# Window attention in pairs: copies placed between exponentials, variances by ScalarE squares with sums, small products at other pairs, indices from one row

## Chip, cores and metric

The kernel runs on one core of a Trainium2 chip. The metric is the device time of one launch in microseconds. Engines are named as in the profile: PE (TensorE), PEld (its weight loads), DVE (VectorE), ACT (ScalarE), POOL (GpSimd), SP (the queue that issues most DMAs).

## What is computed

A network of four layers works on 4 images of 256 channels by 64 x 64 positions, each layer as `x = x + layer(groupnorm(x))`. Layers 2 and 3 are state-space layers and are not touched. Layers 0 and 1 have the same form: a gated scan, then window attention with routing. Cut to the part that matters:

```python
def ssa(x_img, ...):                     # 8 x 8 windows of 8 x 8 positions, 8 heads of 32 channels
    q, k, v = split(xw @ qkv_w.T + qkv_b)
    logit = q.mean(2) * SCALE @ k.mean(2).T
    idx = top_k(logit, 4)                # 4 windows for each window
    k_g, v_g = kv[idx]                   # gathered: 4 x 64 keys and values
    attn = softmax(qh * SCALE @ kh.T)
    out = attn @ vh + lepe(v)            # lepe: a 3 x 3 depthwise convolution
    return out @ wo_w.T + wo_b

def _gn(v, G=32, eps=1e-5):              # v read as (batch, height, width, channels)
    g = v.reshape(B_, H_, W_, G, C_ // G)
    m, s = mean and variance of g over axes (1, 2, 4)
    return ((g - m) / sqrt(s + eps)).reshape(v.shape)
x = x + _L0_conv_ref(_gn(x), ...)
x = x + _L1_conv_ref(_gn(x), ...)
```

The array stands as (4, 256, 64, 64), so the axis that the group norm splits in 32 groups is the last spatial one: a group is a pair of columns over all 256 channels and 64 rows, for each image. A strip of 8 columns has four groups.

## The kernel before

Four images go one after the other. For each, `attention_layers` runs layer 0 and layer 1, and each layer has a scan phase (`scan_phase`), a small routing step and a window phase (`window_phase`). The image `x` stays in on-chip memory as 128 partitions by 2 halves of 4096. It is cut in 8 strips of 8 columns.

The window phase runs 32 pairs of windows, `i` from 0 to 31, with `sj, a = divmod(i, 4)`: strip `sj`, place `a` in it. The order on each engine is the order of the code: there is no scheduler, each engine takes its queue in turn, and semaphores are set where data or buffers demand it. The heads are handled in two halves, `h` 0 and 1, and the steps of one half are:

- `scores(i, h)` (L491): 32 small PE products into the PSUM tile `sc`. The tiles of `h` 0 and 1 alternate over two buffers.
- `smallest(i, h)` (L503): a VectorE minimum over `sc`, 128 x 1024, into `mn`.
- `exps(i, h)` (L514): four ScalarE exponentials of 128 x 256 with row sums, into `pr` and `sm`. A sum is read out by a second small instruction.
- `normalise(i, h)`: a VectorE reciprocal of the sums (L526) and four GpSimd scalings of `pr` (L529).
- `turn(i, h)` (L542): eight PE transposes into two PSUM tiles `pt`, of which there are only two buffers.
- `turned(h, 0)` on VectorE (L553) and `turned(h, 1)` on ScalarE (L555) copy them out to `pts` and so free the buffers.
- `values(i)` (L568): 64 small PE products of a pair into `ov`; `own_rows(i)` (L579) adds them to the image `vimg` on VectorE.

The pairs overlap: in the turn of the loop for pair `i`, PE works on scores of `i` (half 1) and `i + 1` (half 0), transposes of `i - 1` (half 1) and `i` (half 0), and values of `i - 1`. Besides these the loop places, between the steps:

- `project(s, m)` (L202, then `add`, L589) in the pairs with `a` 1 and 2, for the strip before: four PE products of 128 x 512 into the PSUM tile "mm", which has a single buffer in this phase, and a VectorE addition to `x`. Four other pairs (`i` 19, 20, 23, 24) hold a convolution for later queries (`query`) in the same buffer, moved out by ScalarE.
- `taps`: 51 GpSimd steps of the 3 x 3 convolution, two in each pair up to `i` 25. A tap is a product into a tile with tag "sq" (L223) and an addition (L226).
- `gather(i + 3)` and `indices(i + 4)`: eight SP transfers of 128 KB for a pair's keys and values into `kv` (room for four pairs), and two register loads, one for each window, from the routing result `idx` (L456).
- group-norm steps. `mids[i]` run ahead of the reciprocal of half 0, `ends[i]` at the end of the pair. In layer 0 they are the full norm `gn` of strips 0 and 1 for layer 1: sums on VectorE (L143), a PE product (`columns("pm")`, L134), a GpSimd subtraction (`center`, L151), a ScalarE square into a tile with tag "sq" (L159), a VectorE reduction (`reduce`, L163), a PE product (`columns("pv")`), and the scaling on GpSimd (`scale`, L174 and L178). In layer 1 they are `stats`: the same steps up to the variance, for layer 2, with the result kept in `gvar`. The last strip's statistics follow the phase.

The tag "sq" has one buffer, shared by these two lines:

```python
both = norm.tile([P, 2, 8, S], F32, tag="sq", name="tap", bufs=1)                  # L219, a tap
box["sq"] = norm.tile([P, 2, 8 * S], F32, tag="sq", name="gn_sq", bufs=1)          # L156, gn
```

Of the kernel before, what the change touches and what calls it, by code (L numbers as in the profile page):

```python
# [8 lines left out]
F32 = mybir.dt.float32  # L9
# [35 lines left out]
class Net:  # L45
# [33 lines left out]
    def attention_layers(self, x, w_drams, v_drams):  # L79
        tc, nc = self.tc, self.nc  # L80
        with ExitStack() as ctx:
# [40 lines left out]

            def gn(lay, s, psum, eng=nc.gpsimd, var=None):
                xs = x.rearrange("p (c h w) -> p c w h", c=2, w=S)[:, :, strip[s], :]
                box = {}

# [23 lines left out]

                def square():
                    xn = lay["xn"][s].rearrange("p c w h -> p c (w h)")
                    if var is None:
                        box["sq"] = norm.tile([P, 2, 8 * S], F32, tag="sq", name="gn_sq", bufs=1)  # L156
                    else:
                        box["sq"] = xn
                    nc.scalar.activation(box["sq"], xn, AF.Square)  # L159

                def reduce():
# [4 lines left out]

                def scale():
                    pv = box["pv"][:, 0:8]
                    if var is not None:
                        nc.vector.tensor_copy(var, pv.rearrange("p (g t) -> p g t", t=2)[:, :, 0])  # L170
                        return
# [20 lines left out]
                return g[0], both(g[1], g[2]), both(g[3], g[4]), both(g[5], g[6])  # L192


            def stats(s, psum, eng=nc.gpsimd):
                return gn(dict(xn={}), s, psum, eng, self.gvar[:, 4 * s : 4 * s + 4])


            def conv(psum, w, w0, src, m, tag="mm", **kw):
# [239 lines left out]
            def window_phase(lay, work, psum, idx, nxt):  # L439
# [8 lines left out]
                def queue(i, w):  # L448
                    return (nc.scalar, ET.Activation) if i < 2 and w else (nc.sync, ET.SP)

                def indices(i):
                    if i < n_pair:
                        regs[i] = []
                        for w in range(2):
                            p = window(i, w)
                            loads, win = nc.values_load_multi_w_load_instructions(  # L456
                                idx[p : p + 1, 0:TOPK], engines=[queue(i, w)[1]], min_val=0,
                                max_val=NW * NW - 1,
                                skip_runtime_bounds_check_because="places among 64 columns",
                            )  # L460
                            regs[i].append(win)
# [168 lines left out]
                for i in range(n_pair):  # L630
                    sj, a = divmod(i, 4)
                    add = evict = None
                    if i:
                        scores(i, 1)
                        turned(0, 0)
                        turned(0, 1)
                        turn(i - 1, 1)
                        smallest(i, 1)
                    for t in mids.get(i, ()):
                        t()  # L640
                    exps(i, 0)
                    if i == 0:
                        for f in early:
                            f()
# [61 lines left out]
            for i, lay in enumerate(layers):  # L706
# [15 lines left out]
                with tc.tile_pool(name=f"at_c{i}", bufs=1, reuse_waits="tile") as work, tc.tile_pool(  # L722
# [1391 lines left out]
```

## Time and profile before

| what | us |
|---|---|
| timed runs, median of 3 | 11982.6 |
| lowest and highest | 11980.29, 11991.5 |
| the profiled execution | 12008.04 |
| its span | 12006.0 |
| window phase of layer 0, four images, first to last minimum (L503) | 243.1, 244.8, 239.7, 243.8 |
| window phase of layer 1, four images, the same | 262.7, 262.6, 259.5, 264.0 |

The eight window phases take some 2000 us of 12000; the rest is scan phases and the state-space layers. All profile lines below are from one execution. A line of instructions has engine, line, operation, tiles, count, busy time and mean duration; a window line has the stretch, its length, busy time and count of each engine (PE, PEld, DVE, ACT, POOL), then the granted TensorE clock as a share of full speed, the share of the DMA engines and GB/s. A chain line has start, length and what was running; "issue" is time in which nothing that the profile shows was waited for.

### The profile page before, as it was taken

Reading aid. Unit: us, or ns where it says so; the run is one execution under the profiler, and the core shown is the slowest. Engines: PE = TensorE matmul, PEld = TensorE weight load, DVE = VectorE, ACT = ScalarE, POOL = GpSimd, SP = SyncE. Lnnn points to the kernel's source line nnn. Section 1 sums busy time; section 2 is a strip of 40 time slices with the busy share of each in tenths; the row PEclk is TensorE's granted clock in tenths of the full one; section 3 lists DMA queues with packets and bytes.
Section 4 is the critical chain, followed back from the end, with each engine's and each line's share of the span. In section 5 each row is a group of like instructions: output and inputs, shape, how many; then the busy total and the mean of one; then the engine's idle time right before and its main releaser. Section 6 shows DMA issues by size and latency. Waiting matters only on the chain. (4 is left out here: it accounts for less than half of the span.)

```text
span 12006.0 us, 192840 instructions
## 1 busy us (share of the span) xinstructions
PE 10107.7 (84%) x71104; PEld 5773.4 (48%) x71104; DVE 9878.0 (82%) x8386; ACT 6942.4 (58%) x12872; POOL 8890.2 (74%) x6082
## 2 busy tenths in 40 slices
PE   8998887777899788777789988878779998887777
PEld 4554554444455455444445545544444554554444
DVE  6667998998666799889866679989986667998998
ACT  4555554776455555577645555547764555554776
POOL 4666886898466688689846668868974666886897
PEclk9998998999999899899999989989999998998999
DMA  3344544554334455455433435545543343554554
GB/s 98 101 126 131 173 172 147 170 180 160 92 99 125 129 173 174 145 169 182 162 91 101 126 133 173 174 148 170 182 160 90 95 130 131 172 175 147 168 174 155
DMA packets 681294, 1742.11 MB, mean 145 GB/s; under 512 B 87680, under 2 KB 193680, under 8 KB 680096
## 3 DMA queue, kind: packets, MB, share of 16 engines
q1 hardware_dynamic: 675232, 1721.38, 44.5%
q8 instruction: 563, 9.22, 0.3%
q10 hardware_dynamic: 5120, 8.39, 0.3%
q14 instruction: 379, 3.10, 0.1%
HBM read 1601.51 MB, written 94.37 MB: 141 GB/s over the span
## 5 line engine op out<-in xcount | busy, mean ns | idle before, releaser
L958 POOL TENSOR_TENSOR hc<-h,cb 128x1024 f32<-128x1024 f32 x2056 | 4811.7, 2353 | 788.3 <-DVE h L952 349.3
L952 DVE TENSOR_TENSOR_SCAN h<-da,m_state,pb 128x1024 f32<-128x1024 f32 x1248 | 2919.9, 2340 | 163.9 <-DVE pb L946 3.3
L904 PE MATMUL y<-ident,hc 128*128 128x128 f32 x16384 | 2349.9, 291 | 416.7 <-POOL hc L958 347.7
L904 PEld LDWEIGHTS y<-ident,hc 128*128 128x128 f32 x16384 | 2046.9, 151 | 1141.2 <-POOL hc L958 598.6
L946 DVE TENSOR_TENSOR pb<-du,pb 128x1024 f32<-128x1024 f32 x1672 | 2024.3, 1211 | 128.6 <-PE pb L876 126.7
L888 ACT ACTIVATE da<-delta,m_v 128x1024 f32<-128x1024 f32 x1672 | 1899.1, 1141 | 135.2 <-DVE h L952 118.6
L876 PE MATMUL pb<-m_parts,pick 128*128 128x512 bf16 x3312 | 1081.2, 411 | 830.0 <-DVE h L952 771.7
L529 POOL TENSOR_SCALAR pr<-pr,sm,zero 128x256 f32<-128x256 f32 x2048 | 1139.2, 574 | 371.9 <-DVE sm L526 326.4
L876 PEld LDWEIGHTS <-pick 128*128 128x128 bf16 x3312 | 263.7, 101 | 1774.5 <-DVE h L952 971.8
L503 DVE TENSOR_REDUCE mn<-sc 128x4 f32<-128x1024 f32 x512 | 627.0, 1226 | 553.8 <-PE sc L491 553.3
L952 DVE TENSOR_TENSOR_SCAN h<-da,pb 128x1024 f32<-128x1024 f32 x424 | 969.7, 2287 | 55.6 <-DVE pb L946 1.5
L514 ACT ACTIVATE pr<-sc,mn 128x256 f32<-128x256 f32 x2048 | 941.3, 480 | 74.1 <-DMA kv<-kv_dram 57.0
L862 POOL TENSOR_TENSOR bb<-du,bb 128x1024 f32<-128x1024 f32 x376 | 889.2, 2365 | 119.7 <-DMA bb<-m_cd 112.6
L542 PE MATMUL pt_ps<-ident,pr 128*128 128x128 f32 x4096 | 719.3, 301 | 125.9 <-POOL pr L529 111.2
L555 ACT ACTIVATE pts<-pt_ps 128x512 f32<-128x512 f32 x512 | 306.5, 599 | 772.3 <-PE pt_ps L542 771.2
L952 DVE TENSOR_TENSOR_SCAN h<-dap,m_state,bb 128x1024 f32<-128x1024 f32 x288 | 672.1, 2334 | 68.4 <-ACT dap L888 47.9
L202 PE MATMUL conv_ps<-att_y,att_wb 128*128 128x512 f32 x1536 | 684.1, 595 | 4.4 <-DVE gn_mean L149 4.4
L542 PEld LDWEIGHTS pt_ps<-ident,pr 128*128 128x128 f32 x4096 | 482.9, 148 | 310.1 <-POOL pr L529 255.8
L491 PE MATMUL sc<-kv,q_swap 32*64 32x128 f32 x8192 | 602.5, 290 | 3.1 <-DMA kv<-kv_dram 2.7
L888 ACT ACTIVATE dap<-delta,m_v 128x1024 f32<-128x1024 f32 x376 | 419.7, 1116 | 307.8 <-DVE h L952 238.6
L491 PE MATMUL sc<-kv,att_y 32*64 32x128 f32 x7168 | 568.5, 288 | 6.8 <-DVE att_y L270 2.8
L491 PEld LDWEIGHTS sc<-kv,att_y 32*64 32x64 f32 x7168 | 431.3, 140 | 140.1 <-ACT pr L514 78.0
(295 smaller groups left out, 18095.2 us busy)
## 6 DMA issues: line engine op xcount, KB each, us to landing
cb<-m_cd SPq DMA_DIRECT2D x2048, 512.0 KB, 3.9
kv<-kv_dram SPq DMA_DIRECT2D x1984, 128.0 KB, 2.8
bb<-m_cd SPq DMA_DIRECT2D x376, 512.0 KB, 5.3
kv_dram<-kst SPq DMA_DIRECT2D x128, 256.0 KB, 3.5
kv_dram<-vn SPq DMA_DIRECT2D x128, 256.0 KB, 4.1
q_swap<-att_y SPq DMA_DIRECT2D x96, 256.0 KB, 4.1
m_pe<-in_pe_dram SPq DMA_DIRECT2D x32, 512.0 KB, 5.9
out_dram<-yo SPq DMA_DIRECT2D x64, 256.0 KB, 2.5
```

Of the source, the lines that this page charges most:

```text
L202: nc.tensor.matmul(ps, w[:, k, w0 + m * P : w0 + (m + 1) * P], src[:, k], start=(k == 0), stop=(k == 1),)
L491: nc.tensor.matmul(sc[h][b * 64 : b * 64 + 64, r, w, m, :], (own(sj, m) if r == b else swap[sj % 2][:, m])[rows, 2 * a + w], kv[i, w][rows ...
L514: nc.scalar.activation(t[:, g].rearrange("p j r t -> p r j t"), sc[h][:, :, g // 2, g % 2, :].rearrange("p r (j t) -> p r j t", j=2), AF.E ...
L529: nc.gpsimd.tensor_scalar(t[:, g], t[:, g], s[:, g : g + 1], self.zero, ALU.mult, ALU.add)
L542: nc.tensor.transpose(pt[h][j][:, g, :], t[:, g, j].rearrange("p r t -> p (r t)"), self.ident,)
L862: nc.gpsimd.tensor_tensor(pb[i], slots[i][0]["du"], pb[i], ALU.mult)
L876: nc.tensor.matmul(pb[i][:, ss], self.pick[:, n : n + 1].to_broadcast([P, P]), blk["parts"][:, ss], start=True, stop=True,)
L888: nc.scalar.activation(da[i], blk["delta"], AF.Exp, scale=blk["a"](n))
L904: nc.tensor.matmul(blk["y"][:, ss], t[:, ss], self.ident, is_transpose=True, start=(n == 0 and ss.start % NT == 0), stop=(n == DS - 1 and ...
L946: nc.vector.tensor_tensor(pb[i], blk["du"], pb[i], ALU.mult)
L952: nc.vector.tensor_tensor_scan(h[i][:, ss], da[i][:, ss], pb[i][:, ss], state, ALU.mult, ALU.add)
L958: nc.gpsimd.tensor_tensor(hc[i][:, ss], h[i][:, ss], cb[i][:, ss], ALU.mult)
```

## The change

Five things are altered, all of them inside the window phase or at its end.

1. The four exponentials of a half are split in two and two. Two are queued ahead of the copy `turned(h, 1)` on ScalarE, two behind it.
2. `normalise(i, 1)` is placed ahead of `own_rows(i - 1)`, so that the reciprocal stands first on VectorE.
3. `stats` (layer 1) is written anew: after the mean, four ScalarE squares with bias and sum take the place of subtraction, square and reduction; the squares themselves go to a tile with tag "xn" and are not used.
4. The steps of `gn` and `stats` are planned at other pairs.
5. From pair 4 on the indices are loaded from one row `row` with eight entries a pair by one register load. Two transfers ahead of pair 0 make that row by way of DRAM.

```diff
-            def stats(s, psum, eng=nc.gpsimd):
-                return gn(dict(xn={}), s, psum, eng, self.gvar[:, 4 * s : 4 * s + 4])
+            def stats(s, psum):
...
+                def mean():
+                    box["mean"] = self.small.tile([P, 4], F32, tag="gn_mean", name="gn_mean")
+                    nc.vector.tensor_scalar(
+                        box["mean"], box["pm"][:, 0:4], -1.0, None, ALU.mult
+                    )
+
+                def squares():
+                    box["s2"] = self.small.tile([P, 4], F32, tag="gn_s2", name="gn_s2")
+                    sq = norm.tile([P, 2, 8, S], F32, tag="xn", name="gn_sq")
+                    for g in range(4):
+                        two = slice(2 * g, 2 * g + 2)
+                        nc.scalar.activation(
+                            sq[:, :, two], xs[:, :, two], AF.Square,
+                            bias=box["mean"][:, g : g + 1], accum_out=box["s2"][:, g : g + 1],
+                        )
+
+                def variance():
+                    nc.vector.tensor_copy(self.gvar[:, 4 * s : 4 * s + 4], box["pv"][:, 0:4])
+
+                return (
+                    sums, lambda: columns("pm", box["s1"]), mean, squares,
+                    lambda: columns("pv", box["s2"]), variance,
+                )
...
+                row = work.tile([1, NW * NW, TOPK], U32, tag="row", name="row")
+
+                def load_row():
+                    listed = dram.tile([NW * NW, 8], U32, tag="listed", name="listed")
+                    nc.sync.dma_start(listed, idx)
+                    nc.sync.dma_start(
+                        row.rearrange("o (s a) k -> o s a k", a=NW),
+                        listed[:, 0:TOPK].rearrange("(o a s) k -> o s a k", o=1, a=NW),
+                    )
+
                 def indices(i):
-                    if i < n_pair:
+                    if 3 < i < n_pair:
+                        loads, win = nc.values_load_multi_w_load_instructions(
+                            row[0:1, 2 * i : 2 * i + 2, :], engines=[ET.SP], min_val=0,
...
                 for i in range(3):
                     gather(i)
                     indices(i + 1)
+                load_row()
...
                     for s in range(2):
-                        i = 25 + s
-                        plan(gn(nxt, s, lambda: psum), (ends, 22 + 2 * s), (ends, i), (mids, i + 1),
-                             (ends, i + 2), (mids, i + 3), (ends, i + 3), (mids, i + 4))
+                        i = 10 + s
+                        plan(gn(nxt, s, lambda: psum), (ends, i), (ends, i + 1), (mids, i + 2),
+                             (ends, i + 2), (mids, i + 3), (ends, i + 5), (mids, i + 6))
                 else:
                     for s in range(NW - 1):
-                        i = 4 * s + (10 if s < 5 else 7)
-                        plan(stats(s, lambda: psum), (ends, 4 * s + 6), (ends, i), (mids, i + 1),
-                             (ends, i + 2), (mids, i + 3), (ends, i + 3), (mids, i + 4))
+                        i = 4 * s + 6
+                        last = i + 6 if s < 5 else i + 3
+                        plan(stats(s, lambda: psum), (ends, i), (ends, i + 1), (mids, i + 2),
+                             (ends, i + 2), (ends, last), (mids, last + 1))
                 for i in range(n_pair):
                     sj, a = divmod(i, 4)
                     add = evict = None
+                    exps(i, 0, (0, 1))
                     if i:
                         scores(i, 1)
                         turned(0, 0)
                         turned(0, 1)
                         turn(i - 1, 1)
                         smallest(i, 1)
+                    exps(i, 0, (2, 3))
                     for t in mids.get(i, ()):
                         t()
-                    exps(i, 0)
...
+                    exps(i, 1, (0, 1))
                     scores(i + 1, 0)
                     if i:
                         turned(1, 0)
...
                     turn(i, 0)
                     smallest(i + 1, 0)
-                    exps(i, 1)
+                    exps(i, 1, (2, 3))
+                    normalise(i, 1)
                     if i:
                         own_rows(i - 1)
-                    normalise(i, 1)
...
-                        g = stats(NW - 1, lambda: psum, nc.vector)
-                        for t in (left[0], tail[0], left[1], tail[1], g[0], left[2], g[1], g[2],
-                                  left[3], g[3], left[4], *g[4:]):
+                        g = stats(NW - 1, lambda: psum)
+                        for t in (left[0], tail[0], left[1], tail[1], g[0], left[2], left[3], *g[1:]):
                             t()
```

`gn` loses the branch for variances alone (`var`); its own steps stay as they were.

More of the change, by code (lines that the diff above doesn't have):

```diff
@@ L121, in attention_layers, with gn @@
             strip = [slice(s * 8, s * 8 + 8) for s in range(NW)]
-            def gn(lay, s, psum, eng=nc.gpsimd, var=None):
+            def gn(lay, s, psum, eng=nc.gpsimd):
                 xs = x.rearrange("p (c h w) -> p c w h", c=2, w=S)[:, :, strip[s], :]
@@ L154, in square @@
                     xn = lay["xn"][s].rearrange("p c w h -> p c (w h)")
[L155 to L158, printed above, removed]
+                    box["sq"] = norm.tile([P, 2, 8 * S], F32, tag="sq", name="gn_sq", bufs=1)
                     nc.scalar.activation(box["sq"], xn, AF.Square)
@@ L168, in scale @@
                     pv = box["pv"][:, 0:8]
-                    if var is not None:
-                        nc.vector.tensor_copy(var, pv.rearrange("p (g t) -> p g t", t=2)[:, :, 0])
-                        return
                     rstd = self.small.tile([P, 8], F32, tag="gn_rstd", name="gn_rstd")
@@ L192, in gn_four, with columns, sums @@
                 return g[0], both(g[1], g[2]), both(g[3], g[4]), both(g[5], g[6])
-            def stats(s, psum, eng=nc.gpsimd):
-                return gn(dict(xn={}), s, psum, eng, self.gvar[:, 4 * s : 4 * s + 4])
+            def stats(s, psum):
+                xs = x.rearrange("p (c h w) -> p c w h", c=2, w=S)[:, :, strip[s], :]
+                box = {}
+                def columns(tag, part):
+                    box[tag] = psum().tile([P, NT], F32, tag="mm", name=f"gn_{tag}")
+                    nc.tensor.matmul(box[tag][:, 0:4], self.one_gn, part, start=True, stop=True)
+                def sums():
+                    box["s1"] = self.small.tile([P, 4], F32, tag="gn_s1", name="gn_s1")
+                    xr = x.rearrange("p (n w) -> p n w", w=S)[:, :, strip[s]]
+                    nc.vector.tensor_reduce(
+                        box["s1"], xr.rearrange("p n (g t) -> p g n t", t=2), AX.XY, ALU.add
+                    )
[19 more added lines that the diff above has]
+                )
             def conv(psum, w, w0, src, m, tag="mm", **kw):
@@ L449, in queue @@
                     return (nc.scalar, ET.Activation) if i < 2 and w else (nc.sync, ET.SP)
-                def indices(i):
-                    if i < n_pair:
+                row = work.tile([1, NW * NW, TOPK], U32, tag="row", name="row")
[5 more added lines that the diff above has]
+                        listed[:, 0:TOPK].rearrange("(o a s) k -> o s a k", o=1, a=NW),
+                    )
+                def indices(i):
+                    if 3 < i < n_pair:
+                        loads, win = nc.values_load_multi_w_load_instructions(
+                            row[0:1, 2 * i : 2 * i + 2, :], engines=[ET.SP], min_val=0,
+                            max_val=NW * NW - 1,
+                            skip_runtime_bounds_check_because="places among 64 columns",
+                        )
+                        regs[i] = [win[0:TOPK], win[TOPK:]]
+                    elif i < n_pair:
                         regs[i] = []
```

## The prediction

> **What bounds the kernel now.** First the page, then each attention stage alone (the window view), then the chain of waits inside one, then the waits and the timeline. From the page:
>
> ```profile
> PE 10107.7 (84%) x71104; PEld 5773.4 (48%) x71104; DVE 9878.0 (82%) x8386; ACT 6942.4 (58%) x12872; POOL 8890.2 (74%) x6082
> ```
>
> No engine is full, so the price of an edit is a stage's matter. The change touches the eight window phases, two per image: one of layer 0 (251 us here), one of layer 1 (271 us). By the window view, last image, with the granted clock third from the right:
>
> ```profile
> 9219.00:9470.50 251.50, 231.22 (x4576) 165.39 (x4577) 168.76 (x258) 157.91 (x576) 202.60 (x312) 0.94 0.54 152
> 9677.00:9948.50 271.50, 240.16 (x4618) 174.20 (x4619) 180.39 (x277) 161.12 (x581) 207.27 (x313) 0.91 0.49 137
> ...
> 9438.00:9451.70 13.70, 13.70 (x187) 11.92 (x184) 7.87 (x12) 8.51 (x29) 6.44 (x12) 0.50 0.40 121
> ```
>
> A phase runs 32 pairs. 14 carry a projection and four a query convolution; 14 are plain. I take a pair's time from the timeline, between the ends of successive minima (L503) of head half 0: 7.63 us where a convolution runs (7.95 for the first of two), 6.24 us plain. The chain through a convolution pair shows why:
>
> ```profile
> 9408.98 1.08 PE sc L491 x32
> 9410.06 0.02 issue
> 9410.08 1.07 DVE mn L503
> 9411.15 0.08 issue
> 9411.23 0.06 DVE vimg L579
> 9411.29 0.27 issue
> 9411.56 0.18 DVE sm L526
> 9411.74 0.02 issue
> 9411.76 0.02 POOLq L529
> 9411.78 0.12 issue
> 9411.90 2.18 POOL pr L529 x4
> 9414.08 0.04 issue
> 9414.13 0.77 PE pt_ps L542 x5
> 9414.89 1.72 PE conv_ps L202 x4
> ```
>
> This loop closes on itself in 7.63 us: scores, minimum, own_rows (L579, 0.06+0.27), reciprocal, four scalings, transposes, convolution. In a plain pair the 1.72 drops out and GpSimd binds: its timeline has no hole.
>
> ```profile
> 350.60 2.19 POOL L529 TENSOR_SCALAR pr<-pr,sm,zero 128x256 f32<-128x256 f32 x4
> 352.73 1.21 POOL L226 TENSOR_TENSOR vimg<-vimg,tap 128x512 f32<-128x512 f32 x1
> 354.04 2.18 POOL L529 TENSOR_SCALAR pr<-pr,sm,zero 128x256 f32<-128x256 f32 x4
> 356.20 0.77 POOL L223 TENSOR_SCALAR tap<-vimg,att_v,zero 128x512 f32<-128x512 f32 x1
> ```
>
> 8 x 0.54 + 1.19 + 0.77 = 6.27 us. Layer 1 is longer by its variances; its waits name one cause, the PSUM buffer "mm" shared by the small products and the projections (PE waits for the add that reads the projection):
>
> ```profile
> PE gn_pv L134 <- DVE x L589: 6.1, 6, 1.0
> PE gn_pm L134 <- DVE x L589: 5.7, 5, 1.7
> ```
>
> **A. own_rows behind the reciprocal.** It leaves the loop above: 0.06+0.27 = 0.33 us a convolution pair, 7.63 to 7.30. Next late is PE itself: scores 2 x 1.03, values 1.03, transposes 1.03 and 1.33 (with the GpSimd wait), convolution 1.82, 7.27 us together, so 0.33 is the limit. Plain pairs gain nothing (GpSimd). Of 18 such pairs I count 15 in layer 0 and 16 in layer 1, the rest being held by C or B: 5.0 and 5.3 us a phase.
>
> **Exponentials around the copies.** ScalarE now queues e e copy e e. I set the plain pair out from the issue of scores(i,1) at 0. Minimum(i,0) ends at -0.7 and two exponentials (0.45 each) fill ScalarE until 0.22, where it used to wait for the transposes (ready 0.16): the first copy is late by nothing, and sums come 0.9 us earlier, which the reciprocal, behind minimum(i,1) until 2.24, does not use. In the other half, minimum(i,1) ends at 2.33, two exponentials at 3.27, the copy, visible at 3.9, lets values(i-1) go; formerly PE came there at 3.39. Values end 4.93; transposes(i,0) wait for GpSimd's scaling until 5.10 anyway. So 0 us; cover gone, each later us costs one. In a convolution pair values are due at 5.2 and nothing changes.
>
> **B. Variances of layer 1.** Seven strips a phase drop a GpSimd subtraction (L151, 2.47), a VectorE reduction (L163, 1.21) and one ScalarE square (1.08); they get four squares with sums on ScalarE. Four sums-with-exponential cost 4 x 0.45 = 1.8 us, which I take for these equal sizes; ScalarE's load is 4.7 us in 6.24, and after the squares the next exponentials start 0.9 us late while the reciprocal they feed still waits for a minimum: 0. Products and their copies go to pairs whose buffer is free. Size: pairs 0 to 30 sum to 256.4 us in layer 1 against 237.4 in layer 0 (means of four phases); layer 0 holds 10.9 us of its own group norm (pairs 23 and 26 to 30 above their kind: 0.5, 1.3, 0.6, 4.6, 1.9, 2.0), so the excess of the variances is 29.9. What stays: strip sums (L143, 1.22) on VectorE ahead of the copy that frees a transposes' buffer, 1.25 x 6; the last product, still behind an add, 1.3, and its copy 0.2; products on PE in four query pairs 4 x 0.36. Together 10.4; gain 19.5. Bounds: 29.9 if all is hidden, 9.8 if half stays. With A 24.8 a phase, four phases: 99.
>
> **C. Group norm of the next layer, moved from pairs 22-31 to 10-17.** Here I expect a loss. GpSimd's taps run until pair 25, so pairs 10-17 have no GpSimd slack where 27-31 had 2 us each. And the square's output shares its only buffer (tag "sq", L156) with the taps' product (L219): the square at the end of pair 12 must wait until the tap's add (L226) has read that buffer. That add stands behind four scalings; ScalarE is in order, so both exponentials and the copy of pair 13 stand behind it. Pair by pair: strip sums in 11 and 12 +1.8; subtraction 2.47 in the GpSimd-bound pair 12, 2.2 after slack; pair 13: add ends 3.5 us in, square to 4.6, exponentials to 5.5, copy visible 6.1, then half the transposes 0.5, convolution 1.8, scores, values, transposes 3.1: 11.3 instead of 7.3, +4.0; pair 14 the same with the second strip, +4.2; pairs 16 and 17: power 1.64 + scaling 1.90 on GpSimd, 3.6 less slack, +3.2 and +3.0. Sum 18.4. In 13 and 14 PE stands 3.7 us, and the trace halves its clock after waits far shorter: in the 0.50 row above the longest PE gap just before was 1.4 us, and eight transposes took 1.90 instead of 1.03. Bounds for that: 0, or all 5.4 us of PE work behind the wait doubled, in two pairs; I take half, 5.4 in all. 23.8 replaces 10.9: 12.9 lost, 5.0 from A, net -7.9 a phase, four phases -32.
>
> [...]
>
> **D. Tail of layer 1.** The last strip's statistics stand alone after the phase: sums 1.22, left-over reduction 1.12, subtraction 1.88, square 1.06, reduction 1.23, products and copies 1.0 (chain, 9961.8 to 9969.4). Subtraction and two reductions go, the square becomes 2.0: 7.5 to 5.0, 2.5 x 4 = 10.
>
> **E. Indices in one row.** Two transfers on SP at the phase's start, ahead of gather(3); the first must land before the second is issued. Nearest row: a cached 128 KB gather lands 2.8 us after issue, so SP is about 3 us late once. Gather(3) ended at 244.2 for scores at 250: cover 3 us, lands just in time. 0 to 2 us a phase; I take 0.5, minus 4 in all. From pair 4 one register load (0.36 us) less per pair on SP, about 6.2 us busy per pair; hidden, since no steady pair waits for kv.
>
> **Sum.** 99 - 32 + 10 - 4 = 73 us. The profiled execution took 12008.0 (span 12006.0 and 2 around it), giving 11935; it stands 25 us above the median of the timed runs, so 11910.
>
> **Rivals.** (1) The buffer wait of C is short, because the add has run ahead, and the clock stays up: C without 8.2 and without 5.4, four times 13.6 = 54 more: 11855. For: GpSimd idles 1.4 us in some convolution pairs; against: 12 is plain and carries the subtraction. (2) Layer 1 keeps half its excess, because strip sums still hold the transposes' buffer: 4 x 9.8 = 39 less, 11949. (3) Slower: the second copy, now behind two exponentials, holds values. Margin 0.17 us to GpSimd's 5.10. If minima end 1 us later than in my table, as they do wherever VectorE carries more, 14 plain pairs x 8 phases x 1.0 = 112: 12022. For: PE waits are few now, so a late copy shows at once; against: GpSimd binds these pairs and absorbs the first 0.2, and the minimum has nothing ahead of it in most.
>
> **How the numbers follow.** Forecast 0.55 (11870 to 11950), rival 1 0.15, rival 2 0.15, rival 3 0.15. The range 11825 to 11998 takes in rivals 1 and 2 with their bounds and leaves out most of 3. 0.2% (24 us) is what a measurement can tell from no change: faster 0.76 (the first three, less a part of 2), same 0.10, slower 0.14.
>
> **What would show it.** Right: convolution pairs of 7.3 us with L526 directly after L503; layer 1 phases near 247 us and layer 0 near 259; in layer 0 a ScalarE wait of over 3 us before the square at pairs 12 and 13, with pairs 13 and 14 near 11 to 14. Wrong: plain pairs above 6.5 us with PE waiting for the copy (rival 3); layer 0 phases as short as before (rival 1); layer 1 above 257 (rival 2).

## The result and the profile after

The changed kernel takes 11990.42 us (median, 11978.26 to 12002.06); the kernel before, run beside it, takes 11988.55. The ratio is 0.9999, 95% interval 0.9991 to 1.0008: no difference that can be measured. The forecast was 11910, that is 0.994. The profiled execution took 11985.0 us, its span is 11983.3.

From the page of the kernel after, the engines and the group of the exponentials:

```profile
PE 10083.2 (84%) x71104; PEld 5778.2 (48%) x71104; DVE 9833.8 (82%) x8350; ACT 7002.3 (58%) x13096; POOL 8811.5 (74%) x6054
...
L561 ACT ACTIVATE pr<-sc,mn 128x256 f32<-128x256 f32 x2048 | 955.9, 482 | 647.5 <-DVE sm L573 480.9
```

VectorE lost 44 us of work, GpSimd 79, ScalarE gained 60; the span is 23 us shorter than that of before, about what two executions of one kernel differ by. The exponentials now stand idle for 647.5 us, most of it until a reciprocal (L573) is done, against 74.1 before. That looks alarming, but ScalarE is busy for 58% of the span, and such a row does not say whether anyone waited for the exponentials. The window view of the last image's two phases shows what did move:

```profile
9208.30:9465.30 257.00, 232.77 (x4574) 166.93 (x4572) 168.08 (x260) 158.43 (x577) 204.04 (x314) 0.93 0.50 149
9671.80:9934.00 262.20, 233.97 (x4591) 169.01 (x4589) 173.38 (x272) 171.83 (x622) 192.55 (x309) 0.93 0.49 143
```

Layer 0 went from 251.5 to 257.0 us, layer 1 from 271.5 to 262.2 (stretches to the end of the last projection). As means over the four images, pairs 0 to 30 sum to 246.7 us in layer 0 (237.4 before) and 247.5 in layer 1 (256.4 before): +9.3 and -8.9 a phase, which cancel.

What the first edit promised is there. The chain of waits in a quiet convolution pair (start, length, what ran) no longer has own_rows between the minimum (L550, whose 1.07 us are shown as 0.04 and an "issue" of 1.01) and the reciprocal (L573):

```profile
9402.26 1.08 PE sc L538 x32
9403.36 0.04 DVE mn L550
9403.40 1.01 issue
9404.43 0.07 issue
9404.51 0.18 DVE sm L573
9404.69 0.09 issue
9404.78 2.17 POOL pr L576 x4
9406.95 0.04 issue
9407.00 0.77 PE pt_ps L589 x5
9407.76 1.72 PE conv_ps L232 x4
9409.48 1.08 PE sc L538 x32
```

From scores to scores this loop closes in 7.22 us, where it took 7.63. PE is busy for 14.73 of the 15.00 us from 9402 on, so PE now leaves little to gain in these pairs.

What went wrong in layer 1 shows best in one pair. ScalarE's timeline in pair 13 of the first image, without the sums' read-outs, and PE's (the number in brackets is idle time, and what ended it):

```profile
801.65 0.77 ACT L215 ACTIVATE gn_sq<-x,gn_mean 128x256 f32<-128x256 f32 x1
...
803.83 0.76 ACT L215 ACTIVATE gn_sq<-x,gn_mean 128x256 f32<-128x256 f32 x1
...
804.55 0.50 ACT L561 ACTIVATE pr<-sc,mn 128x256 f32<-128x256 f32 x1
...
805.00 0.50 ACT L561 ACTIVATE pr<-sc,mn 128x256 f32<-128x256 f32 x1
...
805.45 0.63 ACT L602 ACTIVATE pts<-pt_ps 128x512 f32<-128x512 f32 x1
```

```profile
806.14 0.91 PE L589 MATMUL pt_ps<-ident,pr 128*128 128x128 f32 x4 [1.17 <-ACT pts L602]
806.84 3.36 PE L232 MATMUL conv_ps<-vimg,att_wb 128*128 128x512 f32 x4
```

Four squares stand from 801.65 to 804.55: 2.9 us, not the 1.8 of the forecast. Behind them come the two exponentials that the change put ahead of the copy (L602), and only then the copy that frees a transposes' buffer. PE waits 1.17 us for it, and then its clock falls: the convolution takes 3.36 us, and the window view gives a granted clock of 1.00 up to 806.39, of 0.54 for the stretch of the convolution, and of 0.95 for the next:

```profile
802.98:806.39 3.41, 2.15 (x39) 1.55 (x39) 1.53 (x3) 3.41 (x14) 2.76 (x4) 1.00 0.44 144
806.10:809.50 3.40, 3.36 (x8) 1.72 (x8) 0.79 (x2) 3.20 (x13) 2.12 (x4) 0.54 0.59 190
809.50:812.90 3.40, 3.40 (x104) 2.51 (x103) 1.60 (x4) 0.28 (x1) 0.98 (x3) 0.95 0.57 152
```

Pair 13 of layer 1 takes 11.2 us as a mean of four images (8.16 before). Pairs 9, 13, 17 and 29, all with four squares queued ahead of them, together grew by 7.7 us a phase; all the others of layer 1 shrank by 16.6. Pairs 21 and 25 have four squares ahead of them too and grew by only 0.1 us each (7.63 to 7.76 and 7.74); the pair before each of these two holds a query convolution and takes longer than a plain one. That this is what spares them was not tested.

The wait does not bring the clock down everywhere. In pair 17, 33 us later, the same copy holds PE for 1.16 us and the convolution takes 1.88 us at full clock. So it is in all four images: the clock falls in pair 13, not in pair 17, and pair 17 takes 9.5 us where pair 13 takes 11.2:

```profile
839.50 0.65 PE L589 MATMUL pt_ps<-ident,pr 128*128 128x128 f32 x4 [1.16 <-ACT pts L602]
839.99 1.88 PE L232 MATMUL conv_ps<-vimg,att_wb 128*128 128x512 f32 x4
...
839.50:842.90 3.40, 3.40 (x44) 1.99 (x48) 0.79 (x2) 3.16 (x13) 2.16 (x5) 1.00 0.70 209
```

In layer 0 the predicted stall is there. GpSimd, ScalarE and PE in pair 13 of the first image:

```profile
336.94 2.17 POOL L576 TENSOR_SCALAR pr<-pr,sm,zero 128x256 f32<-128x256 f32 x4
339.07 1.19 POOL L256 TENSOR_TENSOR vimg<-vimg,tap 128x512 f32<-128x512 f32 x1
...
340.29 1.06 ACT L156 ACTIVATE gn_sq<-att_xn 128x1024 f32<-128x1024 f32 x1 [6.34 <-POOL vimg L256]
341.26 0.46 ACT L561 ACTIVATE pr<-sc,mn 128x256 f32<-128x256 f32 x1
...
342.15 0.59 ACT L602 ACTIVATE pts<-pt_ps 128x512 f32<-128x512 f32 x1
...
342.80 1.12 PE L589 MATMUL pt_ps<-ident,pr 128*128 128x128 f32 x4 [2.01 <-ACT pts L602]
```

The square starts 0.03 us after the tap's add (L256) has ended: ScalarE stood 6.34 us for a scratch buffer that GpSimd was reading, and the exponentials and the copy stood behind it. PE's wait of 2.01 us runs from 340.79 to 342.80. Its clock had been at half since 335.36, 5.4 us before this wait began; the waits before that were of 0.54, 0.59 and 0.21 us:

```profile
331.95:335.35 3.40, 2.06 (x78) 1.36 (x68) 1.94 (x4) 2.00 (x9) 3.40 (x4) 1.00 0.42 128
335.37:345.59 10.22, 7.98 (x52) 5.71 (x52) 4.00 (x6) 5.30 (x18) 7.73 (x10) 0.50 0.50 147
```

### The profile page after: what moved, and what is told of

It reads as the page before. It is cut to its first block, busy times and chain, and to the rows that moved or that the text cites. A ratio compares the mean times of both kernels' runs of the same rounds, so it can differ in the third digit from the quotient of the medians.

```text
span 11983.3 us, 192241 instructions
## 1 busy us (share of the span) xinstructions
PE 10083.2 (84%) x71104; PEld 5778.2 (48%) x71104; DVE 9833.8 (82%) x8350; ACT 7002.3 (58%) x13096; POOL 8811.5 (74%) x6054
## 4 chain that ended last, share of the span: by engine, by line
DVE 23%; PE 23%; ACT 8%; issue 5%; POOL 4%; DMA 1%; SPq 0%; DVEq 0%; POOLq 0%; ACTq 0%
DVE h L1002 13%; DVE pb L996 5%; PE conv_ps L232 4%; PE y L954 4%; PE u_ps L1291 3%; ACT da L938 2%; PE pb L926 1%; PE u_ps L1664 1%; POOL pr L576 1%; PE sc L538 1%; DVE lp L270 1%; PE pt_ps L589 1%; ACT dap L938 1%; PE z_ps L1316 1%; POOL hc L1008 1%
## 5 line engine op out<-in xcount | busy, mean ns | idle before, releaser
L576 POOL TENSOR_SCALAR pr<-pr,sm,zero 128x256 f32<-128x256 f32 x2048 | 1136.5, 569 | 476.8 <-DVE sm L573 475.8
L561 ACT ACTIVATE pr<-sc,mn 128x256 f32<-128x256 f32 x2048 | 955.9, 482 | 647.5 <-DVE sm L573 480.9
L550 DVE TENSOR_REDUCE mn<-sc 128x4 f32<-128x1024 f32 x512 | 627.9, 1228 | 550.0 <-PE sc L538 547.2
L270 DVE SCALAR_TENSOR_TENSOR lp<-vimg,att_v,lp 128x512 f32<-128x512 f32 x616 | 465.4, 756 | 28.1 <-DVE lp L270 1.4
```

The lines of the kernel that those rows point to most:

```text
L561: nc.scalar.activation(t[:, g].rearrange("p j r t -> p r j t"), sc[h][:, :, g // 2, g % 2, :].rearrange("p r (j t) -> p r j t", j=2), AF.E ...
L576: nc.gpsimd.tensor_scalar(t[:, g], t[:, g], s[:, g : g + 1], self.zero, ALU.mult, ALU.add)
```

## The experiments

A negative number in the table is a gain. "Us" is the ratio's distance from 1, times 12000; sums are of pairs 0 to 30, mean of four phases, from the profiled execution. The four phases behind one mean lie 2 to 10 us apart, and e3 and e5, whose layer 0 is the same code, have 236.2 and 233.5 there, so a difference of 2 to 3 us between two sums is not told apart.

| kernel | ratio to before | interval | us | layer 0 | layer 1 |
|---|---|---|---|---|---|
| before | 1 | | | 237.4 | 256.4 |
| after | 0.9999 | 0.9991-1.0008 | -1 | 246.7 | 247.5 |
| e1: before + own_rows | 0.9974 | 0.9965-0.9983 | -31 | 232.5 | 252.0 |
| e2: after - row | 0.9991 | 0.9982-1.0 | -11 | 244.8 | 246.7 |
| e3: e2 + own buffer | 0.9959 | 0.9946-0.9973 | -49 | 236.2 | 247.2 |
| e4: after, squares read in pairs | 0.9965 | 0.9951-0.9978 | -42 | 247.3 | 237.4 |
| e5: e3 + squares read in pairs | 0.9937 | 0.9923-0.995 | -76 | 233.5 | 239.0 |
| e6: e5, `gn` of layer 0 back | 0.9926 | 0.9912-0.9939 | -89 | 232.6 | 239.5 |
| e7: e6, exponentials whole | 0.9907 | 0.9891-0.9922 | -112 | 233.3 | 233.6 |
| e8: e6, squares a pair later | 0.992 | 0.9907-0.9934 | -96 | 232.0 | 236.8 |
| e9: after, exponentials whole | 0.9958 | 0.9944-0.9972 | -50 | 244.6 | 237.5 |
| e10: after, `gn` of layer 0 back | 0.996 | 0.9946-0.9973 | -48 | 231.8 | 249.8 |
| e11: before + row | 1.0011 | 1.0002-1.002 | +13 | 238.7 | 255.7 |
| e12: before + split exponentials | 0.9992 | 0.9983-1.0001 | -10 | 232.3 | 255.6 |

**e1, own_rows alone.** The kernel before with one line moved.

```diff
+                    normalise(i, 1)
                     if i:
                         own_rows(i - 1)
-                    normalise(i, 1)
```

> The kernel before with one edit: the reciprocal of half 1 stands ahead of own_rows. Theory: the 0.33 us (7.63 to 7.22 in the changed kernel's quiet pairs, so up to 0.41) leave the loop of each convolution pair, some 16 a phase: 42 to 52 us less than before, 0.35 to 0.45%. Rival: the shorter pairs of the changed kernel come from the split exponentials, not from this: no change here, convolution pairs stay at 7.63.

Convolution pairs went from 7.63 to 7.29 us, and the quiet plain pairs 7 and 11 of layer 0 from 6.24 to 6.08 and 6.07, which was not forecast. Layer 0 lost 4.9 us a phase, layer 1 4.4 (forecast 5.0 and 5.3). This edit is worth 31 us of the 41 predicted for it, with an interval that reaches to 42.

**e2, no row.** The changed kernel without `row` and its two transfers, with two register loads in every pair as before.

> The changed kernel with the indices loaded as before (no row, no transfers for it). Theory: the two transfers ahead of gather(3) are what makes pairs 2 and 3 of layer 0 8 to 9.5 us instead of 6.5: 5 us a phase in layer 0, 1 to 2 in layer 1, 25 us less than the changed kernel, so some 0.2% faster than before. Rival: these pairs are late because the copies stand behind exponentials while PE's clock is half: no change from the changed kernel.

Pair 2 of layer 0 fell from 8.69 to 6.20 us and pair 3 from 9.31 to 6.61, but the sum of the phase only from 246.7 to 244.8, since other pairs gave part of it back. In time it is about 10 us of the 25 expected, and the intervals of the two kernels overlap.

**e3, a buffer of its own for the square of `gn`,** on top of e2 (the buffer takes the room that the row had).

```diff
-                    box["sq"] = norm.tile([P, 2, 8 * S], F32, tag="sq", name="gn_sq", bufs=1)
+                    box["sq"] = norm.tile([P, 2, 8 * S], F32, tag="gsq", name="gn_sq", bufs=1)
```

> The kernel of e2 with a buffer of its own for the square of the group norm (tag gsq), so that it does not wait for the tap's add. Theory: ScalarE's wait of over 3 us ahead of the square goes; pairs 13 and 14 of layer 0 fall from 15.4 and 12.4 us to about 9 and 8: 9 to 11 us a phase of layer 0, some 40 us less than e2. Rival: GpSimd's subtraction in pairs 12 and 13 holds them, with or without the buffer: under 10 us less than e2, pairs 13 and 14 above 11 us.

Layer 0 fell by another 8.6 us a phase. Pair 13 went from 15.44 to 12.38, pair 14 from 13.19 to 7.87. In ScalarE's timeline the same square of pair 13 now waits for its own input (L151) alone, 1.32 us in place of 6.34:

```profile
338.07 1.06 ACT L156 ACTIVATE gn_sq<-att_xn 128x1024 f32<-128x1024 f32 x1 [1.32 <-POOL att_xn L151]
```

So the shared buffer is shown as the larger part of what `gn` loses at its new place: 8.6 us a phase, where going back to the old place gives 15.0 (e10). In pair 13 most of that is the clock. It takes 11.54 us in the three images in which the clock now stays up, and 14.88 in the fourth, in which it is at half for 10.2 us as in the changed kernel; the waits of 0.54 and 0.59 us that precede the fall there stand in two of the other three images too, so why it falls in some and not in others is open. Pair 17 stays at 14.24; the forecast put it down to GpSimd's own work for the norm, which no run took apart. In the changed kernel PE waits 1.9 us for GpSimd's scalings (L576) there, and then runs at half clock for 6.8 us.

**e4, squares that read pairs of neighbours.** A group is two columns of an image whose columns lie side by side in memory, 64 apart from row to row. The changed kernel walks the long way first; here the two neighbours are innermost. Same elements, same sums.

```diff
+                    sq = sq.rearrange("p c w h -> p (c w h)").rearrange("p (g n t) -> p g n t", g=4, t=2)
+                    xr = x.rearrange("p (n w) -> p n w", w=S)[:, :, strip[s]]
                     for g in range(4):
-                        two = slice(2 * g, 2 * g + 2)
                         nc.scalar.activation(
-                            sq[:, :, two], xs[:, :, two], AF.Square,
+                            sq[:, g], xr[:, :, 2 * g : 2 * g + 2], AF.Square,
```

> The changed kernel with the four squares of layer 1 reading x with the two neighbouring columns as the inner dimension (and writing in that order), where they read one column at a stride of 64 before. Theory: the stride makes a square 0.74 us from start to start instead of the 0.45 of an exponential of the same size; read in this order it falls towards 0.45, and pairs 9, 13, 17 and 29 of layer 1 fall by 2 to 4 us: 30 to 48 us less than the changed kernel. Rival: the length comes from reading on-chip memory for a sum at all, or the sum's read-out: squares stay near 0.74 and nothing moves.

The groups of the kernel after and of e4 in the same stretch of the last image's layer 1, with shapes kept apart (count, busy us, mean ns; the phase of e4 is shorter, so that the stretch takes in two more strips):

```profile
L215 ACT ACTIVATE gn_sq<-x,gn_mean 128x256 f32<-128x256 f32 x24 | 17.8, 774 | 0.0
```

```profile
L216 ACT ACTIVATE gn_sq<-x,gn_mean 128x256 f32<-128x256 f32 x32 | 16.4, 530 | 8.4 <-DVE gn_mean L206 8.4
```

774 ns became 530, start to start 0.73 became 0.505. Four squares now take 2.0 us, and layer 1 fell by 10.1 us a phase; pair 13 went from 11.18 to 8.66, pair 29 from 11.20 to 8.36. One access order of one small instruction is worth 41 us of the changed kernel, where the split stands behind it.

**e5, e3 and e4 together.** 

> The three repairs together: no row, a buffer of its own for the square of layer 0, squares of layer 1 read with two neighbouring columns inside. Theory: they touch different pairs and add up: layer 0 as in e3 (pairs 0 to 30 in 236 us), layer 1 as in e4 less its late pairs 2 and 3 (236 us); about 11930 us where before has 11990, ratio 0.994 to 0.996. Rival: they share slack, and the sum of two repairs is worth no more than the better one: ratio 0.996 or above.

Layer 0 at 233.5, layer 1 at 239.0: the cures act in different phases and add up, within the intervals. The time is 76 us below that of the kernel before.

**e6, `gn` of layer 0 at its old pairs,** with the shared buffer again.

```diff
-                        i = 10 + s
-                        plan(gn(nxt, s, lambda: psum), (ends, i), (ends, i + 1), (mids, i + 2),
-                             (ends, i + 2), (mids, i + 3), (ends, i + 5), (mids, i + 6))
+                        i = 25 + s
+                        plan(gn(nxt, s, lambda: psum), (ends, 22 + 2 * s), (ends, i), (mids, i + 1),
+                             (ends, i + 2), (mids, i + 3), (ends, i + 3), (mids, i + 4))
```

> The kernel of e5 with the group norm of layer 0 back at pairs 22 to 31 and the square in the shared buffer again. Theory: the move to pairs 10 to 17 costs more than it frees even without the buffer wait, because GpSimd has slack only from pair 26 on: layer 0 as in e1 (232 us against 236), 10 to 20 us less than e5. Rival: late pairs with group norm cost as much as early ones once the buffer is its own: within 8 us of e5.

Once the buffer is cured, the two places are nearly equal (233.5 and 232.6 us a phase; e3, with the same layer 0 as e5, has 236.2). The ratio fell by 13 us, which fits the 10 to 20 of the first theory, but the intervals of e5 and e6 overlap and the phases do not show it.

**e7, the exponentials in one piece,** on top of e6: the four calls of `exps` with halves became the two of the kernel before, behind the copies.

> The kernel of e6 with the four exponentials of a half in one piece behind the copy, as before. Theory: the split is worth 0.06 us in a convolution pair (7.22 against 7.28) and nothing in a plain pair: 5 to 10 us more than e6. Rival (the slower one of the prediction): the second copy behind two exponentials holds values, so undoing the split makes it faster by 10 us or more, plain pairs first.

Layer 1 fell by a further 5.9 us a phase, layer 0 stayed. e7 is the fastest version: 11885.03 us, 0.9907 of the kernel before, and faster than both kernels of the case. Its interval and that of e6 overlap by a little, the pairs do not: 13, 17 and 29 of layer 1 take 7.94, 8.02 and 7.91 us against 8.73, 8.60 and 8.59. The loss of 5 to 10 us that the first theory expected did not come. The windows of the last image of e7:

```profile
9136.60:9382.00 245.40, 224.58 (x4576) 161.48 (x4578) 168.82 (x260) 157.54 (x576) 203.61 (x313) 0.97 0.56 156
9588.50:9839.00 250.50, 230.63 (x4610) 168.63 (x4612) 174.77 (x271) 166.29 (x623) 192.61 (x308) 0.94 0.54 149
```

**e8, squares one pair later,** on top of e6.

```diff
-                             (ends, i + 2), (ends, last), (mids, last + 1))
+                             (ends, i + 2 + (s < 5)), (ends, last), (mids, last + 1))
```

> The kernel of e6 with the four squares of strips 0 to 4 of layer 1 at the end of the first projection pair in place of the plain pair before it. Theory: ScalarE has 2.5 us to spare in a projection pair of 7.2 and 1.5 in a plain one of 6.2, and four squares need 2.0: pairs 13 and 17 fall from 8.6 to 7.7 and pairs 10, 14, 18 rise by less than 0.5: 10 to 15 us less than e6. Rival: the squares are late wherever they stand, since the exponentials of the next pair stand behind them: the loss moves to pairs 10, 14 and 18, within 5 us of e6.

Pairs 13 and 17 stayed at 8.48 and 8.47 us (8.73 and 8.60 in e6), though the squares had left the ends of 12 and 16. That theory fell, and the loss did not move to pairs 10, 14 and 18 either (7.89, 7.21 and 7.21): what is left in these pairs with the split on does not come from the place of the squares. The time is that of e6. The trace shows where it comes from. Just ahead of pairs 13 and 17, in all four images of e8, PE stands 0.54 to 0.55 us in the values for the copy (L586) that now follows two exponentials; with the exponentials whole (e7) no such wait of over 0.25 us is left in any window phase. In the second image, ahead of pair 13:

```profile
3746.52 0.98 PE L599 MATMUL ov_ps<-pts,kv 128*32 128x64 f32 x52 [0.55 <-ACT pts L586]
```

**e9, the changed kernel with the exponentials in one piece.** Only the split is undone; squares stay slow.

> The changed kernel with only the split undone: four exponentials in one piece behind the copy. Theory: where squares stand ahead, the split puts the copy that frees the transposes' buffer behind two exponentials more, so pairs 9, 13, 17 and 29 of layer 1 lose 0.5 to 2 us by it, and pairs 13 and 14 of layer 0 about 0.9 each; convolution pairs go from 7.22 to 7.28. Without the split 20 to 35 us less than the changed kernel, 11960 to 11970 where before has 11990. Rival: the split is neutral, e7 was chance: within 10 us of the changed kernel.

Layer 1 fell by 10.0 us a phase, as much as by e4, and the time by about 50 us, more than the 20 to 35 expected. Pairs 13, 17 and 29 are back at 8.2, 8.2 and 8.1 us; pair 9 stays at 9.7 (10.0 with the split), so its loss is not the split's. ScalarE in pair 13 of the first image, now with the copy (L602) directly behind the four squares, then PE:

```profile
803.49 0.77 ACT L215 ACTIVATE gn_sq<-x,gn_mean 128x256 f32<-128x256 f32 x1
...
804.20 0.63 ACT L602 ACTIVATE pts<-pt_ps 128x512 f32<-128x512 f32 x1
804.68 0.52 ACT L561 ACTIVATE pr<-sc,mn 128x256 f32<-128x256 f32 x1
```

```profile
804.89 0.66 PE L589 MATMUL pt_ps<-ident,pr 128*128 128x128 f32 x4 [0.20 <-ACT pts L602]
805.38 1.88 PE L232 MATMUL conv_ps<-vimg,att_wb 128*128 128x512 f32 x4
```

PE waits 0.20 us instead of 1.17 and the convolution takes 1.88 instead of 3.36: the squares take as long as before, but no exponentials come between them and the copy, and the clock stays up. So the loss is squares plus two exponentials, and taking out either part removes most of it.

**e10, the changed kernel with `gn` of layer 0 at its old pairs** (the diff of e6 alone).

> The changed kernel with only the group norm of layer 0 back at pairs 22 to 31. Theory: pairs 13, 14 and 17 of layer 0 fall to 8, 7.2 and 8, pairs 26 to 30 rise to 9 to 10: layer 0 from 246.8 to about 238 us, 35 us less than the changed kernel. Rival: with the row's late pairs 2 and 3 still there, the earlier end of layer 0's tail hides it: under 15 us.

Layer 0 fell by 15.0 us a phase, to 231.8, and the time by about 48 us, more than the 35 expected.

**e11, the row alone,** on the kernel before: `load_row`, and one register load from pair 4 on.

> The kernel before with the indices in one row as its only change (row written behind the listed pairs and read back, one load of eight entries at the pair that needs them first). If the row's later first gather is a loss that stays: the gather of the third pair is issued 3 to 4 us later, pairs 2 and 3 of layer 0 go from 6.9 and 6.4 us to 8 to 9.5 us, the sum of pairs 0 to 30 of layer 0 is 4 to 6 us larger and that of layer 1 up to 2 us larger, and the whole is 12 to 30 us longer than before. If the phase gives the time back later (the version after without the row came out only 2 us a phase shorter): pairs 2 and 3 lose as said, but the sum of layer 0 is at most 2 us larger and the whole lies within 8 us of the kernel before.

In the whole it costs 13 us (2 to 24). Pairs 2 and 3 of layer 0 grew by 1.9 and 1.2 us, the phase by 1.3, so the first theory holds for the total and the second for the phase. The price agrees with e2, which is the same edit taken out; a phase's 1.3 us is less than these sums can tell apart.

**e12, the split alone,** on the kernel before: four calls of `exps`, two ahead of each copy and two behind.

> The kernel before with the exponentials split around the copies as its only change. If the split costs only where squares stand ahead of it (four squares in a row, then two exponentials, then the copy): the plain pairs stay within 0.05 us of before, pairs 9, 13, 17 and 29 of layer 1 within 0.5 us, both sums of pairs 0 to 30 within 3 us of before, and the whole within 10 us. If a copy that stands behind two exponentials costs by itself: plain pairs 0.2 us or more longer, each phase 5 us or more longer, and the whole 30 us or more longer.

Neither sum of a phase grew; plain pairs stay at 6.24 and convolution pairs gain 0.08 us (7.55). Pair 13 of layer 1 is 8.27 us (8.16): there its square is a single one of 1.06 us. Layer 0 fell by 5.1, more than the 3 us expected; the convolution pairs explain little over 1 of that, and the rest is no more than the images of one kernel differ by. The copy does hold the values in quiet plain pairs (0.41 us in pairs 7 and 11 of layer 0), but these pairs do not get longer by it. The split alone is neutral, and in layer 1 it costs 10 us a phase where four squares stand ahead of it.

## Why the prediction was wrong

**The step that failed** is the one on the exponentials and the squares. The prediction said of the split: "So 0 us; cover gone, each later us costs one", and of the squares: "Four sums-with-exponential cost 4 x 0.45 = 1.8 us, which I take for these equal sizes", with a further 0 for the exponentials behind them. Two things were wrong with these zeros. The size: a square over columns 64 apart took 774 ns against 488 of an exponential with the same count of elements (0.73 and 0.45 start to start), and 530 ns with two neighbours innermost (e4). And the accounting: each zero was worked out with the other edit absent. The split was costed in pairs where nothing stands ahead of the exponentials, the squares by looking only at the reciprocal that the next exponentials feed, not at the copy that follows them on ScalarE. Put together, squares 2.9, exponentials 0.9 and the copy 0.6 make 4.4 us in a row, 1.17 more than PE can spare, and where the clock then halves, as in pair 13, that adds 1.5 us to the convolution alone. e12 shows the split alone at no cost, e9 the squares without the split 10.0 us a phase cheaper, e4 the split with shorter squares 10.1 cheaper. Four phases make 40 us, more than half of the 72 between the gain of 73 that was forecast and the 1 that was measured. The squares' own length is most of the rest: with the exponentials whole, layer 1 is another 3.9 us a phase shorter in e7 than in e9, of which the row has some 0.8 (e2).

**A, own_rows: right.** 0.33 us a convolution pair was forecast, 0.34 measured (e1), and PE, the next limit that was named, is busy for 98% of the quiet stretch after the change. The 0.16 us of the quiet plain pairs were not forecast.

**B, variances: right in what it removes, wrong in what it adds.** The forecast for A and B in layer 1 was 24.8 us a phase; the change gave 8.9. With the squares' cures and the exponentials whole (e7) it is 22.8, so the gain had been there and was spent again within the same phase. The pairs where the buffer "mm" had been waited for did get short: pair 14 went from 8.95 to 7.21 us and 16 from 10.74 to 7.01.

**C, the norm of layer 0: right on the buffer, not on the clock, and close in its sum partly by luck.** The buffer of the tag "sq" and the tap's add are as told. The clock is not: in pair 13 it had halved before the wait that the forecast makes it fall by, in all four images; only in pair 14 does it fall behind the wait, of 3.0 us there, or in one image within it. Pairs 11 to 18 grew by 20.8 us (23.8 was forecast for this work) and pairs 23 to 30 shrank by 11.6, part of that by A (10.9 forecast without it). Single pairs were further off: 13 took 15.4 us where 11.3 and 2.7 for the clock were forecast, 16 did not grow at all, 17 grew by 5.7 instead of 3.0, and these misses partly cancel. The total of layer 0 was forecast at -7.9 a phase and came to -9.3. e10 gives back 15.0, where the forecast's loss was 12.9.

When the clock falls was read in the forecast off one row, in which it halved with a longest PE gap of 1.4 us just before. In pair 13 of layer 1 it fell with a wait of 1.17 us, a wait that the forecast did not have. But such a wait is not always enough: pair 17 keeps a full clock after 1.16 us, and in e9 pair 9 of layer 1 keeps it after 1.93 us in the first image and loses it after 1.77 us in the second. So the forecast's way, to read a fall off the length of one wait, is too simple, and what decides is not settled here. The low stretch of pair 13 in layer 1 lasts about 3.4 us (0.54 over 3.40 us above, 0.95 in the next); the one in layer 0 lasts 10.2 us.

**D, the tail: mis-sized.** 2.5 us a phase were forecast, 1.4 came: from the end of the last addition to `m_pe`, 9.6 us before and 8.2 after. The forecast's own list does not give its 2.5: with the subtraction and two reductions gone and the square at 2.0, 7.5 becomes 4.2, not 5.0. The four squares take 2.9 us, not 2.0, and behind them the load of an activation table, which used to run beside VectorE's last reduction, stands in the chain. It runs beside the last product and its copy to `gvar`, which is done at 9953.69, so of its 1.28 us at most the last 0.46 are added. With short squares (e7) the tail is 7.3 us, 2.3 less than before. The chain, then the copy in VectorE's timeline:

```profile
9950.55 2.29 ACT gn_sq L215 x7
9952.85 0.02 issue
9952.86 1.28 ACT L1234
9954.15 0.01 issue
9954.16 0.35 ACT m_dev L1234
```

```profile
9953.53 0.16 DVE L221 COPY gvar<-gn_pv 128x4 f32<-128x4 f32 x1 [3.65 <-PE gn_pv L195]
```

**E, the row: mis-sized.** SP's queue and PE's waits in the first phase, after:

```profile
240.38 0.48 SPq L485 DMA_DIRECT2D listed<-idx  x1
242.06 0.82 SPq L486 DMA_DIRECT2D row<-listed  x1
242.95 0.40 SPq L115 DMA_DIRECT2D att_wa<-in_l_w_dram  x1
243.56 2.52 SPq L516 DMA_DIRECT2D kv<-kv_dram  x4
```

```profile
PE sc L538 <- DMA kv<-kv_dram: 2.1, 2, 1.6
```

The gather is issued 3.9 us later than before (239.70), not "about 3", and lands after the scores want it; none of these waits were there before. The cover of 3 us was misread: 244.2 is where issues ended, not landings. In the kernel before, the seven transfers issued from 239.7 to 244.2 took 6.3 us to land, not 2.8, so the one issued at 243.78 came in at about 250, the very time that the forecast gives for the scores (count, size, median us to landing):

```profile
kv<-kv_dram SPq DMA_DIRECT2D x7, 128.0 KB, 6.3
```

e2 and e11 put the price at 10 to 13 us, 1.2 to 1.6 a phase, inside the stated bounds of 0 to 2 but three times the 0.5 that was taken.

**The sum.** 4 x (8.9 - 9.3) = -2 us of gain from the pairs and 4 x 1.4 = 6 from the tail: 4 us, where the comparison measured 1, give or take 10. For e7 the same account, with its tail, gives 4 x (4.1 + 22.8 + 2.3) = 117 against a measured 112.

**The rivals.** Rival 1 (a short buffer wait) is excluded by the 6.34 us and by e10. Rival 2 had the right sign but another cause: the excess of layer 1 did not stay, a new one came. Rival 3 had the mechanism, a copy behind two exponentials that PE waits for, in the wrong place: the plain pairs it named have the wait but did not grow (e12), four of the pairs with squares ahead did. The split's price was therefore 40 us by e9 (31 by the growth of those four pairs, 7.7 x 4), not 112.

**Open.** What makes the clock fall in one pair and not in another with the same wait was not settled. Why the row costs 3.1 to 5.2 us in pairs 2 and 3 of layer 0 (e11, e2) but only 1.3 to 1.9 in its whole phase was not traced.

## What to carry to other kernels

When two edits put work on the same in-order engine, cost them in the pair where they meet: walk its queue from the first added instruction to the next one that frees a buffer, and ask who waits for that. Take an instruction's price from a row with the same operation, memory and access order, not from one with the same count of elements (774 ns here against 488); for a strided read, see whether the innermost step can be made the short one (530 ns here against 774). And before a step is moved, look at the tag of its scratch buffer as well as at its engine: the shared single buffer here kept ScalarE waiting for GpSimd for 6.34 us.

## What the runs showed of the hardware

- A ScalarE square with sum over 256 f32 elements of on-chip memory took 774 ns when neighbours in the walk were 64 elements apart, and 530 ns with two contiguous ones innermost; 0.73 and 0.505 us from one start to the next. An exponential with sum over 256 elements of PSUM took 488 ns, 0.45 from start to start.
- TensorE's clock halved within 0.5 us of the end of a wait of 1.17 us (pair 13 of layer 1, four images of four): in the first image the next four 128 x 512 convolution products took 3.36 us instead of 1.88. With a wait of 1.14 to 1.18 us (pair 17, none of four) it stayed full, and so it did after one of 1.93 us in pair 9 (e9, first image) and one of 0.20 us in pair 13 (e9, first image). In pair 13 of layer 0 it was down 5.4 us before the wait of 2.01 us (first image).
- An activation table load of 1.28 us ran beside VectorE's last reduction of 1.22 us before the change and is not in that run's chain of waits; after it, behind the last square, at most its last 0.46 us were added.
